# A four-layer graph network on one core: small products of TensorE cut into 64x64 blocks, one batch to a row half

## The chip, the cores and the metric

The kernel runs on one core of a Trainium2 chip. TensorE multiplies matrices into PSUM, VectorE and ScalarE work element by element, GpSimd and the sync engine (SP) issue most of the DMAs. The metric is the device time of the whole kernel in microseconds (us). Everything is fp32, except for masks in bf16.

## The reference

The input x has 8 batches of 2048 nodes with 64 features, and adj is one 2048x2048 matrix that all layers share. Each layer adds its result to its input and normalizes over the 64 features:

```python
x = _layernorm(x + _L0_gnn_ref(x, adj, embedding, weight, bias))   # x, A x, 2 A A x - x; weights per node
x = _layernorm(x + _L1_gnn_ref(x, adj, a))                         # attention, masked by adj, then elu
x = _layernorm(x + _L2_gnn_ref(x, adj, W, b))                      # (A + I)(x W^T + b) / row sum
x = _layernorm(x + _L3_gnn_ref(x, adj, iv, W1, b1, W2, b2, 0))     # three steps, below
```

A step of layer 3 forms `effects = adj @ v`, then `h = relu(concat(v, effects) @ W1.T + b1)` and `v = h @ W2.T + b2`. Four products by 64x64 matrices, or by a matrix of that size, matter here: layer 1's turn-back from features-by-nodes to nodes-by-features with its sum of weights, layer 2's W, the part of layer 3's step that prepares the input of the product with adj, and layer 3's last product with W2.

## The kernel before

Two batches lie side by side in the 128 columns or partitions: a *pair* p has 2 x 64 features, and there are four pairs (NPAIR). Nodes are cut into 16 tiles of 128 (NT) and into four *chunks* of 512 nodes (NCH, four tiles each, TPC). A sweep over adj is a product of a pair with the whole matrix: for each chunk, 16 products of 128x128 with 512 columns, summed in one PSUM tile `acc`.

Since a pair holds two batches, a product of 64x64 weights over its 128 partitions is written with a block-diagonal matrix of 128x128: the weights twice on the diagonal, zeros elsewhere. Such matrices are `w2bd` (layer 2), `w31e` and `ge` (layer 3's input), `w32c` (layer 3's last), and `back` (layer 1's turn-back: the identity, with two more columns that pick each batch's sum). The data are the stationary operand and the small matrix is the moving one. Each is used a chunk at a time:

- `finish` turns layer 1's result back, from `po`, which L889 fills: PSUM tile `pf`, 130 moving columns, two chunks per half of a pair
- `layer2_tail`: PSUM tile `ps_emb`, then VectorE scales, adds and normalizes
- `u_chunk`: PSUM tile `ps_u`, copied or added to a bias into the next sweep's source
- `last_chunk`, and `last_half` at the very end: PSUM tile `ps_v`, added to layer 3's result, normalized, stored

All of them go through `multiply` (L408 in the profile), which writes either one product with 128 output partitions (`PE`, the full form) or two with 64 each that run in two column tiles of the array (`PE columns`), by the form that the array is in. Layer 1's attention (`weights`, L889, `po`) always uses the column form. Layer 0's products (`second_pass`, L660, `yp`) use the row form (`PE rows`): 64 partitions of contraction, one batch to a row half, into the two halves of their PSUM tile.

The order of all instructions is fixed when the program is built. Each task is a Python generator that yields the engine that it needs next and the events that it waits for. `Plan` holds a clock for each engine, costs each piece by formulas (`mm`, `dve`, `act`), and always takes the task that could begin first, with an offset from the table `BACK` that is looked up by the task's name and pair. `Plan.run` adds `SWITCH` when TensorE's form changes. So costs and offsets shape the order on all engines, and the chip then runs that order, each engine waiting on semaphores. PSUM holds rings of tiles: `acc` (2), `pp` (2, all small products), `po` (1).

The main order on TensorE: two sweeps of layer 0 with `second_pass` between their products, then layer 2 and layer 3 of pairs 0 to 3 in turn, while layer 1 of the later pairs runs beneath them. The products of joined pairs use sums of quarters of adj (`joint_step`). SP fetches the tiles of adj into six buffers ahead of TensorE (`fetch`, L277).

Of the kernel before, what the change touches and what calls it, by code (L numbers as in the profile page):

```python
# [9 lines left out]
F32 = mybir.dt.float32  # L10
# [27 lines left out]
class Plan:  # L38
# [11 lines left out]
    FORMS = ("PE", "PE rows", "PE columns", "PE any")  # L50
    SWITCH = 0.2
# [4 lines left out]
        ("add_terms", 0): -3.73,  # L56
        ("h_evict", None): 0.94,
        ("keep", None): -0.94,
        ("last_chunk", None): -8.34,
        ("layer1", None): -0.21,  # L60
        ("mask_of_tile", None): -0.03,
        ("scores", 0): -0.81,
        ("scores", 2): 0.25,
        ("stacks", None): -0.5,
        ("start_chunk", None): -0.38,
        ("sweeps", None): 0.12,
# [29 lines left out]
    def either(self):  # L96
        return "PE" if self.form == "PE rows" else self.form
# [62 lines left out]
def mm(cols, n=1):  # L160

    return n * max(4 * cols / 2390, 0.224)
# [15 lines left out]
def resnorm_d4_kernel(  # L178
# [124 lines left out]
    blocks = ("w2bd", "w31v", "w31e", "w32c")  # L303
    w2bd, w31v, w31e, w32c = (const.tile([P, P], F32, name=n) for n in blocks)
    w32bd_t, w32bd_k = st_ring.take([P, 8, P], "w32bd")
    w32bd = w32bd_t[:, 0, :]
    for t in (a4, w2bd, w31v, w31e, w32bd, w32c):
        nc.vector.memset(t, 0.0)
# [6 lines left out]
    def constants():  # L315

        yield "PE", [40.0]
        nc.sync.dma_start(emb_sb, emb.rearrange("(t p) d -> p t d", p=P))
        nc.sync.dma_start(bias_sb, bias0)
        nc.sync.dma_start(embT, emb_t)  # L320
        halves = [slice(0, C), slice(C, P)]
        for k, w in enumerate((wk0, wk1, wk2)):
            for h in halves:
                nc.sync.dma_start(w[h, :], w0[k * C : (k + 1) * C, :])
        for k in range(2):
            for e in range(2):
                nc.sync.dma_start(a4[halves[e], 2 * k + e : 2 * k + e + 1], a1[halves[k], :])
        yield "PE", [70.0]
        nc.vector.tensor_tensor(wk0, wk0, wk2, ALU.subtract)
        nc.vector.tensor_scalar_mul(wk2, wk2, 2.0)  # L330
        plan.run("DVE", 2.0)
        plan.start(0, embedding_bias())
        yield "PE", [180.0]
        for t, src in (
            (w2bd, w2t),
            (w31v, w31t[0:C, :]),
            (w31e, w31t[C:P, :]),
            (w32bd, w32t),
            (w32c, w32t),
        ):  # L340
            for h in halves:
                nc.sync.dma_start(t[h, h], src)
        nc.sync.dma_start(b2b, b2.to_broadcast([P, C]))
        nc.sync.dma_start(b32b, b32.to_broadcast([P, C]))
        for h in halves:
            nc.sync.dma_start(b31b[h, :], b31)
            nc.sync.dma_start(b32c[h, :], b32.rearrange("o c -> c o"))
        nc.sync.dma_start(ivc, iv)
        yield "PE", [260.0]
        plan.start(0, weights_of_l23())  # L350
        for p in range(2, NPAIR):
            yield "SP", [(270.0, 430.0)[p - 2]]
            for c in range(NCH):
                load_x(p, c, nc.sync)
                at["x", p] = plan.dma("SP", 256)
# [4 lines left out]
    back = const.tile([P, P + 2], F32, name="back")  # L360
    nc.vector.tensor_copy(back[:, 0:P], ident)
    nc.vector.tensor_copy(back[:, P : P + 2], ident[:, C - 1 :: C])
    for e in range(2):
        rows = slice(e * C, (e + 1) * C)
        last = slice(e * C + C - 1, e * C + C)
        nc.vector.tensor_scalar_add(back[rows, last], ident[rows, last], -1.0)
# [4 lines left out]
    ge = const.tile([P, P], F32, name="ge")  # L371
# [38 lines left out]

    def embedding_bias():
        yield "PE", [pp_ring]
        pe, k = pp_ring.take([P, NT, C], "ps_eb")
        for t in range(NT):
            nc.tensor.matmul(
                pe[:, t, :], lhsT=embT[:, t * P : (t + 1) * P], rhs=bias_sb, start=True, stop=True
            )
        done = plan.run("PE", mm(C, NT))
        eng = yield EITHER, [done, e_ring]
        sb, ke = e_ring.take([P, NT, C], "eb_sb")  # L420
        copy(eng, sb, pe)
        done = plan.run(eng, cost(eng, 1024), done)
        pp_ring.give(k, done)
        e_ring.give(embT_k, plan.free["PE"])
        for e in range(2):
            nc.gpsimd.dma_start(eb[:, :, e, :], sb)
            done = plan.dma("DMA", 512, done)
        e_ring.give(ke, done)
        at["eb"] = done

    def weights_of_l23():
# [3 lines left out]
        for w, blocks in ((w2bd, 2), (w32c, 2), (b2b, 1), (b32b, 1)):  # L435
            mean = tiny([P, 1], "w_mean", 2)
            nc.vector.tensor_reduce(mean, w, AX.X, ALU.add)
            nc.vector.tensor_scalar_mul(mean, mean, 1.0 / C)
            for e in range(blocks):
                rows = slice(e * C, (e + 1) * C) if blocks == 2 else slice(0, P)  # L440
                block = w[rows, e * C : (e + 1) * C]
                nc.vector.tensor_scalar(block, block, mean[rows], None, ALU.subtract)
# [26 lines left out]
        for i, dst in enumerate((gv, ge, ceb)):  # L469
            nc.scalar.copy(dst, pw[:, i * P : (i + 1) * P])  # L470
        nc.scalar.activation(b31n, pw[:, 3 * P : 3 * P + 1], AF.Identity, bias=b31b)
# [54 lines left out]
    def layer_norm(v, n, after, centered=False):  # L526
# [4 lines left out]
        if not centered:  # L531
            yield "DVE", [after]
            s = tiny([P, nb], "ln_s", 4)
# [12 lines left out]
        vs = tiny([P, nb], "ln_v", 4)  # L546
# [5 lines left out]
        r = tiny([P, nb], "ln_r", 4)  # L552
        nc.scalar.activation(r, vs, AF.Ln)
        nc.scalar.activation(r, r, AF.Exp, scale=-0.5)
        rr = tiny([P, nb], "ln_rr", 2)
# [350 lines left out]
    def finish(p, h, po, kpo, xc):  # L906
# [11 lines left out]
        for f in range(2):  # L918
            yield "PE", [got, pp_ring]
            pp, k = pp_ring.take([P, 2, CW], "pf")  # L920
            pp = pp.rearrange("p b n -> p (b n)").rearrange("p (t n) -> p t n", n=256)
            for j in range(TPC):
                multiply(
                    pp[:, j, 0 : P + 2],
                    lhsT=poT[:, f, j * P : (j + 1) * P],
                    rhs=back,
                    start=True,
                    stop=True,
                )
            t_pe = plan.run("PE any", mm(P + 2, TPC), got)  # L930
            if f == 1:
                pt_ring.give(kt, t_pe)
            yield "DVE", [t_pe, hp_ring]
            rd = tiny([P, TPC, 2], "rd", 3)
            nc.vector.reciprocal(rd, pp[:, :, P : P + 2])
            hp, kh = hp_ring.take([P, CW], "hp")
            nc.vector.tensor_tensor(
                hp.rearrange("p (t e c) -> p t e c", e=2, c=C),
                pp[:, :, 0:P].rearrange("p t (e c) -> p t e c", c=C),
                rd.unsqueeze(3).to_broadcast([P, TPC, 2, C]),  # L940
# [65 lines left out]
    def h_evict(p, s, c, pa, ka, done):  # L1006
# [11 lines left out]
        if s < 2:  # L1018
            queue2.append(lambda: u_chunk(p, c, ge, u_of(p, s + 1), ceb, s + 1, done))
        else:  # L1020
            queue2.append(lambda: last_chunk(p, c, done))
# [9 lines left out]
    def layer2_tail(p, c, z, kz, done, ring=yt_ring):  # L1031
        yield "PE", [done, pp_ring]
        pe, k = pp_ring.take([P, TPC, P], "ps_emb")
        for j in range(TPC):
            multiply(
                pe[:, j, :], lhsT=z[:, j * P : (j + 1) * P], rhs=w2bd, start=True, stop=True
            )
        done = plan.run("PE any", mm(P, TPC), done)
# [4 lines left out]
        for j in range(TPC):  # L1043
            t = c * TPC + j
            nc.vector.scalar_tensor_tensor(
                v[:, j, :], pe[:, j, :], rdeg[:, t : t + 1], SX[p][:, t, :], ALU.mult, ALU.add
            )
# [8 lines left out]
    def start_chunk(p, c, v, done):  # L1056
# [21 lines left out]
        yield from u_chunk(p, c, w31e, u_of(p, 0), None, 0, done)  # L1078

    def u_chunk(p, c, w, dst, bias, s, done):  # L1080
# [4 lines left out]
        yield "PE", [done, pp_ring, *room]  # L1085
        pu, k = pp_ring.take([P, TPC, P], "ps_u")
        for j in range(TPC):
            multiply(
                pu[:, j, :], lhsT=SH_of[p][:, c * TPC + j, :], rhs=w, start=True, stop=True
            )  # L1090
        done = plan.run("PE any", mm(P, TPC), done)
        if bias is None:
            eng = yield EITHER, [done]
            copy(eng, dst[:, tiles(c), :], pu)
        else:
            eng = yield "DVE", [done]
            nc.vector.tensor_tensor(
                dst[:, tiles(c), :], pu, bias.unsqueeze(1).to_broadcast([P, TPC, P]), ALU.add
# [5 lines left out]
    def last_chunk(p, c, done):  # L1104
        yield "PE", [done, pp_ring]
        pv, k = pp_ring.take([P, TPC, P], "ps_v")
        for j in range(TPC):
            multiply(
                pv[:, j, :], lhsT=SH_of[p][:, c * TPC + j, :], rhs=w32c, start=True, stop=True
            )  # L1110
        done = plan.run("PE any", mm(P, TPC), done)
# [7 lines left out]
        nc.vector.tensor_tensor(v, v, pv, ALU.add)  # L1119
# [4 lines left out]
    def last_half(p, c, f, a, pa, done, token):  # L1124
# [13 lines left out]
        yield "PE", [done, pp_ring]  # L1138
        pv, k = pp_ring.take([P, 2, P], "ps_v")
        for j in range(2):  # L1140
            multiply(pv[:, j, :], lhsT=h[:, j, :], rhs=w32c, start=True, stop=True)
        done = plan.run("PE any", mm(P, 2), done)
# [4 lines left out]
        nc.vector.tensor_tensor(v, v, pv, ALU.add)  # L1147
# [469 lines left out]
```

## Time and profile before

| | |
|---|---|
| runs, us | 2055.12, 2055.51, 2056.45; median 2055.51 |
| profiled execution: span, us | 2054.9 (0.6 under the median; the page gives no other time for it) |
| TensorE busy | 2013.2 us, 98% of the span |
| VectorE busy | 1472.5 us, 72% |
| ScalarE busy | 975.7 us, 47% |
| GpSimd busy | 310.1 us, 15% |
| DMA | 522.81 MB moved, mean 254 GB/s |
| granted TensorE clock | 0.996 on average |

A line of the profile names the line of the kernel, the engine, the operation, the tile written and the tiles read, the shapes and the count. L408 is the helper `multiply`, so products are told apart by the PSUM tile. An fp32 product of the program appears as two MATMUL records, each with a weight load (LDWEIGHTS). `128*128` before the shapes are the active rows and columns of the array: `64*128` is the row form, `128*64` the column form. A record's length includes the time until its result is through, so records overlap; the distance between starts is the rate. A group's idle time is put down to what ended it.

### The profile page before, as it was taken

Reading aid. Unit: us, or ns where it says so; the run is one execution under the profiler, and the core shown is the slowest. Engines: PE = TensorE matmul, PEld = TensorE weight load, DVE = VectorE, ACT = ScalarE, POOL = GpSimd, SP = SyncE. Lnnn points to the kernel's source line nnn. Section 1 sums busy time; section 2 is a strip of 40 time slices with the busy share of each in tenths; the row PEclk is TensorE's granted clock in tenths of the full one; section 3 lists DMA queues with packets and bytes.
Section 4 is the critical chain, followed back from the end, with each engine's and each line's share of the span. In section 5 each row is a group of like instructions: output and inputs, shape, how many; then the busy total and the mean of one; then the engine's idle time right before and its main releaser. Section 6 shows DMA issues by size and latency. Waiting matters only on the chain. (4 is left out here: it accounts for less than half of the span.)

```text
span 2054.9 us, 22213 instructions
## 1 busy us (share of the span) xinstructions
PE 2013.2 (98%) x7835; PEld 889.4 (43%) x7835; DVE 1472.5 (72%) x1906; ACT 975.7 (47%) x1786; POOL 310.1 (15%) x491
## 2 busy tenths in 40 slices
PE   8999999999999999999998999999999999999998
PEld 3444444443343443444333343453344554444444
DVE  2215666999899999979999989999989832121214
ACT  0014444288778546767773846623767521000002
POOL 3220111122222331222211101001101000000000
PEclk9999999999999999999999999999999999999999
DMA  9897776676657789967778779779777677888886
GB/s 297 285 306 257 285 274 231 214 225 174 166 156 234 185 282 324 282 224 272 206 219 318 246 244 347 247 257 359 245 273 259 224 249 262 267 270 267 265 283 197
DMA packets 205714, 522.81 MB, mean 254 GB/s; under 512 B 22290, under 2 KB 29074, under 8 KB 201490
## 3 DMA queue, kind: packets, MB, share of 16 engines
q1 hardware_dynamic: 151570, 352.60, 50.5%
q0 software_dynamic: 51920, 167.74, 27.5%
q8 instruction: 62, 1.02, 0.2%
q10 hardware_dynamic: 2112, 1.05, 0.2%
q14 instruction: 50, 0.41, 0.1%
HBM read 488.61 MB, written 64.16 MB: 269 GB/s over the span
## 5 line engine op out<-in xcount | busy, mean ns | idle before, releaser
L408 PE MATMUL acc<-a,SX 128*128 128x512 f32 (+1 forms) x1372 | 493.6, 597 | 11.4 <-DMA SX<-in_x 6.9
L408 PE MATMUL acc<-a,SB 128*128 128x512 f32 (+2 forms) x1120 | 375.9, 588 | 3.3 <-DMA a<-a_plus_i 2.7
L870 ACT ACTIVATE e<-e,sv 128x1024 f32<-128x1024 f32 x256 | 280.7, 1153 | 70.6 <-DVE e L862 67.8
L408 PEld LDWEIGHTS acc<-a,SX 128*128 128x128 f32 (+1 forms) x1372 | 192.5, 170 | 269.5 <-issue 255.0
L684 ACT ACTIVATE terms<-yp,emb_sb 128x128 f32<-128x128 f32 x896 | 243.0, 396 | 133.8 <-PE yp L660 128.3
L862 DVE TENSOR_TENSOR e<-s1b,mk 128x2048 f32<-128x2048 f32 x128 | 290.1, 2283 | 7.6 <-PE po L889 4.2
L784 DVE CUSTOM_DVE_ANT_0 junk<-s2b,mr 128x2048 bf16<-128x2048 f32 x128 | 292.6, 2286 | 2.3 <-DMA mr<-by_row 0.5
L875 DVE TENSOR_TENSOR e<-e,mb 128x2048 f32<-128x2048 f32 x128 | 290.6, 2284 | 4.1 <-ACT e L870 3.9
L878 ACT ACTIVATE e<-e 128x2048 f32<-128x2048 f32 x128 | 245.7, 1926 | 90.6 <-DVE e L875 89.8
L889 PE MATMUL po<-e,SX 128*64 128x512 f32 x1024 | 232.5, 595 | 3.0 <-ACT e L878 3.0
L408 PEld LDWEIGHTS acc<-a,SB 128*128 128x128 f32 (+1 forms) x1120 | 147.3, 164 | 194.9 <-issue 186.8
L408 PE MATMUL acc<-a,SA 128*128 128x512 f32 (+1 forms) x416 | 176.4, 598 | 4.5 <-DMA a<-in_adj_t 4.5
L857 POOL DMA_DIRECT2D mk<-by_col x128 | 70.8, 560 | 497.9 <-DVE e L862 446.8
L660 PE MATMUL yp<-SH,xgT 64*128 64x512 f32 x512 | 137.2, 613 | 3.4 <-ACT terms L684 3.3
L696 DVE TENSOR_TENSOR terms<-terms 128x512 f32<-128x512 f32 (+1 forms) x176 | 130.0, 739 | 12.0 <-ACT terms L684 7.6
L889 PEld LDWEIGHTS po<-e,SX 128*64 128x64 f32 x1024 | 72.7, 137 | 150.4 <-issue 139.8
L660 PE MATMUL yp<-wk,xgT 64*128 64x512 f32 x512 | 131.8, 592 | 0.0
L660 PE MATMUL yp<-SH,y2T 64*128 64x512 f32 x512 | 131.2, 589 | 0.0
L408 PEld LDWEIGHTS acc<-a,SA 128*128 128x128 f32 (+1 forms) x416 | 70.0, 183 | 90.4 <-issue 87.5
L408 PE MATMUL acc<-a,ut 128*64 128x512 f32 (+1 forms) x272 | 86.4, 593 | 1.4 <-DVE wk L1356 1.4
L408 PE MATMUL acc<-a,t 128*128 128x512 f32 x192 | 85.3, 592 | 0.0
L771 POOL DMA_DIRECT2D mr<-by_row x64 | 34.6, 542 | 294.3 <-DVE mx L784 253.7
(255 smaller groups left out, 1716.0 us busy)
## 6 DMA issues: line engine op xcount, KB each, us to landing
a<-in_adj_t SPq DMA_DIRECT2D x384, 512.0 KB, 5.9
a<-a_plus_i SPq DMA_DIRECT2D x88, 512.0 KB, 5.2
mr<-by_row POOLq DMA_DIRECT2D x64, 512.0 KB, 5.8
mk<-by_col POOLq DMA_DIRECT2D x128, 256.0 KB, 5.8
a<-sb SPq DMA_DIRECT2D x40, 512.0 KB, 4.4
a<-sc SPq DMA_DIRECT2D x40, 512.0 KB, 4.5
a<-sd SPq DMA_DIRECT2D x40, 512.0 KB, 5.1
a<-sa SPq DMA_DIRECT2D x40, 512.0 KB, 4.3
```

The costliest lines, as they stand in the source:

```text
L408: nc.tensor.matmul(out[h], lhsT=lhsT[:, h], rhs=rhs, skip_group_check=True, **kw)
L660: nc.tensor.matmul(yp[:, e, :], lhsT=v[rows, cs], rhs=w[rows, hs], start=(k3 == 0), stop=(k3 == 2),)
L684: nc.scalar.activation(batches(terms[0][:, dd, :]), term, AF.Copy, scale=weight)
L696: nc.vector.tensor_tensor(a, a, b, ALU.add)
L771: nc.gpsimd.dma_start(mk, by_row[t])
L784: nc.vector.tensor_tensor_reduce(out=junk, in0=s2b[e][0], in1=masks[t][0], scale=1.0, scalar=LOWEST, op0=ALU.add, op1=ALU.max, accum_out=m ...
L857: nc.gpsimd.dma_start(mk, by_col[jt // 2][:, jt % 2, h * HALF : (h + 1) * HALF])
L862: nc.vector.tensor_tensor(e, s1b[0], mk.unsqueeze(1).to_broadcast([P, 2, HALF]), ALU.add)
L870: nc.scalar.activation(e[:, i, :], e[:, i, :], AF.Prelu, bias=sv[:, 2 + i, jt : jt + 1], alpha=ALPHA)
L875: nc.vector.tensor_tensor(e, e, mb[0], ALU.add)
L878: nc.scalar.activation(e, e, AF.Exp)
L889: nc.tensor.matmul(po[i * C : (i + 1) * C, f, :], lhsT=SX[p][:, t, i * C : (i + 1) * C], rhs=e[:, i, f * CW : (f + 1) * CW], start=(t == 0 ...
```

## The change

The four kinds of small product no longer use block-diagonal matrices. The matrix is kept twice, one below the other, as [128, 64] (`w2q`, `w31q`, `w32q`, `geq`, and `back` with 65 columns), one copy for each batch's 64 partitions. The new helper `quarters` multiplies in blocks of 64x64: for each tile of 128 nodes, four products, with e the batch (the row half of the array) and f the half of the nodes (the column half). Each batch writes its own half of the PSUM tile, so the evictions read views split by batch. The plan has a new form, `PE quarters`, at 0.112 us for each tile of nodes, the cost of a change of form is set to 0.1 instead of 0.2, the table `BACK` has new offsets, most of them by pair, and some small rings of the norm are deeper.

```diff
-    FORMS = ("PE", "PE rows", "PE columns", "PE any")
-    SWITCH = 0.2
+    FORMS = ("PE", "PE rows", "PE columns", "PE quarters", "PE any")
+    SWITCH = 0.1
...
     BACK = {
-        ("add_terms", 0): -3.73,
-        ("h_evict", None): 0.94,
...
-        ("last_chunk", None): -8.34,
...
+        ('add_eb', 2): 7.7,
+        ('add_terms', 0): -34.15,
...
+        ('mask_of_tile', 2): 24.71,
...
+        ('z_and_v', 3): -21.09,
     }
...
     def either(self):
-        return "PE" if self.form == "PE rows" else self.form
+        return self.form if self.form == "PE columns" else "PE"
...
-    blocks = ("w2bd", "w31v", "w31e", "w32c")
-    w2bd, w31v, w31e, w32c = (const.tile([P, P], F32, name=n) for n in blocks)
+    w31v, w31e = (const.tile([P, P], F32, name=n) for n in ("w31v", "w31e"))
+    w2q, w31q, w32q, geq = (const.tile([P, C], F32, name=n) for n in ("w2q", "w31q", "w32q", "geq"))
...
-            (w2bd, w2t),
             (w31v, w31t[0:C, :]),
             (w31e, w31t[C:P, :]),
             (w32bd, w32t),
-            (w32c, w32t),
         ):
             for h in halves:
                 nc.sync.dma_start(t[h, h], src)
+        for t, src in ((w2q, w2t), (w31q, w31t[C:P, :]), (w32q, w32t)):
+            for h in halves:
+                nc.sync.dma_start(t[h, :], src)
...
+    def quarters(out, source, w, width=C):
+
+        n = source.shape[1] // P
+        for j in range(n):
+            for e, f in ((0, 0), (1, 1), (0, 1), (1, 0)):
+                rows = slice(e * C, (e + 1) * C)
+                nc.tensor.matmul(
+                    out[f * C : (f + 1) * C, e, j * width : (j + 1) * width],
+                    lhsT=source[rows, j * P + f * C : j * P + (f + 1) * C],
+                    rhs=w[rows],
+                    start=True,
+                    stop=True,
+                    skip_group_check=True,
+                )
+
+    def quartered(n):
+
+        return 0.112 * n
...
-        for w, blocks in ((w2bd, 2), (w32c, 2), (b2b, 1), (b32b, 1)):
+        for w in (w2q, w32q, b2b, b32b):
...
-        for i, dst in enumerate((gv, ge, ceb)):
+        for i, dst in ((0, gv), (2, ceb)):
             nc.scalar.copy(dst, pw[:, i * P : (i + 1) * P])
+        for e in range(2):
+            block = slice(e * C, (e + 1) * C)
+            nc.scalar.copy(geq[block, :], pw[block, P + e * C : P + (e + 1) * C])
...
-            s = tiny([P, nb], "ln_s", 4)
+            s = tiny([P, nb], "ln_s", 6)
...
-            yield "PE", [got, pp_ring]
+            yield "PE quarters", [got, pp_ring]
             pp, k = pp_ring.take([P, 2, CW], "pf")
-            for j in range(TPC):
-                multiply(
-                    pp[:, j, 0 : P + 2],
-                    lhsT=poT[:, f, j * P : (j + 1) * P],
-                    rhs=back,
...
+            quarters(pp, poT[:, f, :], back, C + 1)
...
-        yield "PE", [done, pp_ring]
-        pe, k = pp_ring.take([P, TPC, P], "ps_emb")
-        for j in range(TPC):
-            multiply(
-                pe[:, j, :], lhsT=z[:, j * P : (j + 1) * P], rhs=w2bd, start=True, stop=True
-            )
-        done = plan.run("PE any", mm(P, TPC), done)
+        yield "PE quarters", [done, pp_ring]
+        pe, k = pp_ring.take([P, 2, CW], "ps_emb")
+        quarters(pe, z, w2q)
+        done = plan.run("PE quarters", quartered(TPC), done)
...
-        pu, k = pp_ring.take([P, TPC, P], "ps_u")
-        for j in range(TPC):
-            multiply(
-                pu[:, j, :], lhsT=SH_of[p][:, c * TPC + j, :], rhs=w, start=True, stop=True
-            )
-        done = plan.run("PE any", mm(P, TPC), done)
+        pu, k = pp_ring.take([P, 2, CW], "ps_u")
+        quarters(pu, SH_of[p][:, tiles(c), :].rearrange("p t n -> p (t n)"), w)
+        pu = pu[:, :, 0 : TPC * C].rearrange("p e (t c) -> p e t c", c=C)
+        to = by_batch(dst[:, tiles(c), :])
+        done = plan.run("PE quarters", quartered(TPC), done)
...
-        nc.vector.tensor_tensor(v, v, pv, ALU.add)
+        nc.vector.tensor_tensor(by_batch(v), by_batch(v), pv, ALU.add)
```

The products of `last_chunk` and `last_half` change in the same way as `u_chunk`'s.

## The prediction

> **What bounds the kernel now.** I read first the page's busy times and slices, then the busy time of each 100 us, then TensorE's own waits, and last the order of time at a few small products and at changes of form.
>
> ```profile
> PE 2013.2 (98%) x7835; PEld 889.4 (43%) x7835; DVE 1472.5 (72%) x1906; ACT 975.7 (47%) x1786; POOL 310.1 (15%) x491
> ...
> DVE  2215666999899999979999989999989832121214
> ```
>
> TensorE works 98% of the span, so it sets the end. VectorE is nearly as full from slice 8 to 31 (about 400 to 1640 us), and idle after that. So an edit to VectorE's work counts only in the middle, and an edit to TensorE's counts everywhere, as long as VectorE keeps up there. Per 100 us:
>
> ```profile
> 1400.00:1500.00 100.00, 95.53 (x413) 34.46 (x413) 96.37 (x60) 64.71 (x52) 12.97 (x24) 1.00 0.86 306
> ...
> 1700.00:1800.00 100.00, 100.00 (x282) 48.18 (x281) 21.80 (x42) 9.43 (x19) 0.00 (x0) 1.00 0.81 267
> ```
>
> The columns are busy us of TensorE, its weight loads, VectorE, ScalarE, GpSimd, then TensorE's clock and the DMA share. From 1000 to 1500 TensorE loses 14.5 us, the most of any such stretch; from 1700 to 2000 it loses none. Its own waits from 1000 to 1500 are split between adjacency tiles (7.2 us) and results of ScalarE and VectorE (7.2 us in six rows), of which the largest are:
>
> ```profile
> PE acc L408 <- DMA a<-in_adj_t: 4.1, 3, 1.8
> PE acc L408 <- DMA a<-a_plus_i: 3.1, 3, 1.5
> PE po L889 <- ACT e L878: 3.0, 2, 1.8
> ```
>
> Now the price of a small product and of a change of form. In the timeline of TensorE the columns are start, length, what it is, and the count; each fp32 product of the program is two MATMUL records per tile of the array.
>
> ```profile
> 1366.56 1.05 PE L408 MATMUL ps_u<-ge,SH 128*128 128x128 f32 x8
> 1367.45 2.31 PE L408 MATMUL acc<-a,SB 128*128 128x512 f32 x5
> ...
> 795.75 1.04 PE L408 MATMUL ps_emb<-w2bd,z 128*64 128x128 f32 x16
> 796.63 1.89 PE L408 MATMUL acc<-a,SX 128*64 128x512 f32 x8
> ...
> 502.68 0.58 PE L408 MATMUL ps_sv<-a,xT 128*64 128x4 f32 x16
> ...
> 435.51 1.45 PE L408 MATMUL acc<-a,SB 128*128 128x512 f32 x3
> 436.90 0.70 PE L660 MATMUL yp<-SH,xgT 64*128 64x512 f32 x2
> ...
> 438.72 1.02 PE L660 MATMUL yp<-SH,y2T 64*128 64x512 f32 x4
> 439.67 1.55 PE L408 MATMUL acc<-a,SX 128*128 128x512 f32 x3
> ...
> 515.94 1.45 PE L408 MATMUL acc<-a,SA 128*128 128x512 f32 x3
> 517.32 1.94 PE L889 MATMUL po<-e,SX 128*64 128x512 f32 x8
> ```
>
> A chunk of four tiles takes 0.89 us in the full form (1366.56 to 1367.45) and 0.88 in the column form (795.75 to 796.63). The last three pairs are changes of form. Three records of acc are 0.429 us apart (1.45 less one record's 0.592, halved), so the rows' first record was due at 436.80 and came at 436.90, and its pair lasts 0.70 where later pairs last 0.59: entering rows costs 0.10 + 0.10 = 0.20 us. Back into full: due at 439.58, came at 439.67, and three records take 1.55 where they took 1.45: again 0.20. Into columns: due 517.23, came 517.32, and eight records take 1.94 where they take 1.89 without a change: 0.145. So each form has to let the last one end and then shows its first weight load, 0.10 for 128 columns and 0.05 for 64.
>
> **The chunks.** By the groups of TensorE kept apart by shape, ps_u has 288 full and 192 column records, ps_emb 80 and 96, ps_v 72 and 112, pf 88 and 80; at 8 and 16 records that is 66 full and 30 column chunks, 96 in all (two of layer 3's last come as halves, so 97 visits). They cost 66 x 0.89 + 30 x 0.88 = 85.1 us. The new chunk has 16 products of 64x64x64, 32 records. No row shows four tiles at once. The nearest is ps_sv above: 64-column weights, two tiles at once, almost no moving columns; its fifteen starts take 0.58 - 0.195 (one record) = 0.385, and a steady round of two takes 0.0585 by their start times, so one load of 64 columns takes a round. The moving side, half of a 128-column record's 0.111, is 0.055 and hides beneath it. Bounds: four tiles a round give 8 rounds, 0.468 us; two a round, as in every row here, give 16 rounds, 0.936. I take the first: rows (yp) and columns (po) each run their two tiles with starts 0.007 apart (the pair of yp at 436.90 lasts 0.70, one record 0.693), the new blocks combine the two, and the two row halves write different halves of the PSUM tile, as yp's do. 96 x 0.468 = 44.9, a gain of 40.2 us.
>
> The Trainium skill (TensorEngine Tiling, Instruction Overhead) speaks against it: a matmul has about 60 cycles of overhead, so a moving side of 64 should not be tiled further. Its page TensorE: Matmul & The Clock Gate (Wait — 56ns, not 53.3ns?) gives a floor of about 25 ns from start to start; by that a chunk is an estimated 0.80 us, 96 of them cost 32 us more than I count, and the change would lose about 15. The ps_sv row, 0.385 over fifteen starts, cannot tell this floor from its two-tile rounds; starts 0.007 apart in yp say that it isn't one for neighbouring tiles.
>
> **The changes of form.** Before, a chunk takes the form that stands (only rows are left for full), so most change nothing. After, every visit enters and leaves. Keeping the order of before, the 97 visits are 85 runs of neighbouring chunks: 85 entries x 0.145 = 12.3; 61 exits to full or rows x 0.20 = 12.2; 23 to columns x 0.145 = 3.3; less 8 changes that stood there already (1.6). That costs 26.2 us. The rest is 40.2 - 26.2 = 14.0 us gained: some 3 before 1000 us, 7.5 to 1640, 3.5 after. An isolated chunk between full products gains only 0.89 - 0.468 - 0.345 = 0.08.
>
> **The rest of the edits.** The evictions keep their 512 elements a partition. Their views are split by batch; the row of hp<-pf,rd, already split four ways, has 691 ns against 687 of the contiguous sum with ps_v, so nothing, covered by VectorE's 74 us idle from 400 to 1600 us; without that cover 64 times 4 ns is 0.3 us. Set-up: two block loads more on SP (0.48 to 0.59 us each at 183.7), ahead of the next adjacency tiles; at most 1.2 us if TensorE waited for exactly these, and I take none, since SP stood idle for 22 us before them. ScalarE gets one small copy more at about 262 us, VectorE two subtractions of 0.25 and two memsets fewer. Deeper rings of the norm's small tiles let more norms be open and cost no instruction.
>
> **The order.** The new table of offsets rewrites the order on every engine, and the trace can't show it. Best: the 7.2 us of waits for ScalarE and VectorE go, and some twenty visits stand next to another (0.345 each), together -14. Worst: TensorE loses in each 100 us from 1000 to 1600 what it lost in 1400 to 1500 (4.5), 27 where it lost 14.5: +12.5. I take -3: the plan now counts a change of form as 0.1, the rows say 0.145 to 0.20, so TensorE runs behind its plan by some 20 us in all and finds results ready more often. For tiles from HBM nothing changes.
>
> **Sum.** 2054.9 is the span of the profiled execution, 0.6 under the median of the runs, and I count against the median: 2055.5 - 14.0 - 3 = 2038.5.
>
> **Rivals.** (1) Fewer than four tiles at once, or a floor for each matmul. A chunk loses from 0.89 - 26.2/96 = 0.61 us up, that is below three tiles a round; at two, 96 x 0.468 = 44.9 more: 2083. For it: no row with more than two; against: the starts 0.007 apart. (2) VectorE becomes the bound up to 1640 us: what is gained there is given back, only 3.5 us remain, 2052, no change that can be told (within 0.2%, 4 us, is about that). For: 96% busy in the window of 1400 us; against: its 74 us idle. (3) Four at once, but the new order makes TensorE wait, +12.5 instead of -3, and as many more form changes as it gained in clustering is lost on row products: about 2060. For: 0.1 in the plan is too low; against: it makes TensorE late, not early. (4) The order brings all of its 14: 2027, or still more visits side by side, down to 2015.
>
> **How the numbers follow.** The forecast with its own range 2026 to 2049 has 0.54; more than that by the order (4) 0.13; no change (2) 0.08; slower by the order (3) 0.08; tiles not at once (1) 0.17. Faster 0.67, same 0.08, slower 0.25. Four cases in five lie between 2016 and 2076, short of the worst of (1).
>
> **What would show it.** Right: a chunk in 64*64 records, 32 of them, within about 0.5 us of its first start, four starts within 0.03; about 0.145 lost before it and 0.2 after it; VectorE's evictions at their old 687 to 691 ns; TensorE's busy time about 14 us down, its idle not up. Wrong: 0.8 us or more from the first 64*64 start to the last; TensorE's idle over 55 us; VectorE without idle from 1000 to 1640. The forecast falls with the first of these.

## The result and the profile after

The changed kernel takes 2072.04 us (median, 2069.01 to 2073.29) where the kernel before takes 2055.32 beside it: a ratio of 1.0084, 95% interval 1.0062 to 1.0107. It is slower by about 17 us; the forecast was 17 us faster. The profiled execution took 2073.19 us, with a span of 2071.4. From the page:

```profile
span 2071.4 us, 25804 instructions
...
PE 2008.1 (97%) x9623; PEld 855.2 (41%) x9623; DVE 1471.7 (71%) x1903; ACT 976.9 (47%) x1788; POOL 309.5 (15%) x491
...
DVE  2215756998799999989999989999989721111124
```

TensorE is busy 5.1 us less than before (2013.2). But the span less the busy time is now 63.3 us, where it was 2054.9 - 2013.2 = 41.7: 21.6 more, and 21.6 - 5.1 = 16.5 is the whole loss. VectorE's row of slices and its busy time are nearly those of before, so VectorE was not made slower. The busy time per stretch (columns as in the prediction) says where the idle time lies:

```profile
1400.00:1500.00 100.00, 92.96 (x439) 35.30 (x441) 98.09 (x63) 64.99 (x54) 14.59 (x27) 1.00 0.82 290
1700.00:1800.00 100.00, 96.80 (x441) 43.25 (x440) 19.89 (x37) 8.88 (x19) 0.00 (x0) 1.00 0.79 257
1800.00:1900.00 100.00, 96.73 (x405) 42.65 (x404) 16.54 (x25) 5.63 (x9) 0.00 (x0) 1.00 0.79 257
```

In 1400 to 1500 TensorE loses 2.6 us more than before. From 1700 to 2000, where it had lost nothing, it now loses 3.2 in each 100 us, while VectorE is busy 20%: it waits for an engine that has little to do. TensorE's own waits from 1640 us to the end name what it waits for (total, times, longest):

```profile
PE acc L452 <- DVE u L1419: 4.9, 6, 0.9
PE acc L452 <- DVE u L1425: 4.7, 6, 0.8
PE ps_v L469 <- ACT h_o L1198: 1.1, 1, 1.1
PE acc L452 <- DVE u3t L1432: 0.8, 1, 0.8
PE acc L452 <- DVE c L1194: 0.5, 1, 0.5
```

Before, the same stretch has two waits, 2.0 us in all:

```profile
PE ps_v L408 <- ACT h_o L1135: 1.4, 1, 1.4
PE acc L408 <- DVE c L1131: 0.6, 1, 0.6
```

L1419 is `x_of` and L1425 is `z_and_v`, the subtractions on VectorE in layer 3's joint steps of pairs 2 and 3. One such place in the timeline, with a chunk of `ps_u` ahead of it:

```profile
1741.65 0.59 PE L452 MATMUL acc<-a,t 128*128 128x512 f32 x1
...
1742.17 0.69 PE L469 MATMUL ps_u<-geq,SH 64*64 64x64 f32 x32
...
1742.80 7.13 PE L452 MATMUL acc<-a,u3t 128*128 128x512 f32 x16
...
1749.97 0.69 DVE L1419 TENSOR_TENSOR u<-acc,u 128x512 f32<-128x512 f32 x1 [6.34 <-PE acc L452]
...
1750.71 7.13 PE L452 MATMUL acc<-a,u3t 128*128 128x512 f32 x16 [0.78 <-DVE u L1419]
...
1757.96 0.69 DVE L1419 TENSOR_TENSOR u<-acc,u 128x512 f32<-128x512 f32 x1 [7.29 <-PE acc L452]
...
1758.70 5.42 PE L452 MATMUL acc<-a,SB 128*128 128x512 f32 x12 [0.85 <-DVE u L1419]
```

Two things are to be read here. First the chunk: its 32 records of 64*64 take 0.52 us from the start of the last full record to their first start (0.429 was due, so 0.09 goes to letting the array empty), and the next full record starts 0.63 later. By the start times of the records the 32 lie within 0.477 us; three of every four gaps between neighbours are 7 ns or less, and the mean is 15.4 ns. So four blocks do run at once. The second full record of acc comes 0.105 us late (0.534 after the first instead of 0.429), its weight load exposed. A visit that stands alone costs 0.823 against 0.89 before.

Second, the wait. `acc` has two tiles. At 1742.80 a product of 16 records fills one; it is read by VectorE at 1749.97 for 0.69 us; only then does the next product start, at 1750.71, and the next one waits for `x_of` in the same way. Three products in a row use one and the same tile, while the other one is not used. The waits for `z_and_v` are alike: there TensorE adds a product to the tile that VectorE has only just read. The twelve make 9.6 us.

The end has changed, too. The last product of TensorE and what follows:

```profile
2057.36 0.46 PE L469 MATMUL ps_v<-w32q,h_o 64*64 64x64 f32 x16 [1.12 <-ACT h_o L1198]
...
2060.18 1.13 ACT L614 ACTIVATE ln_sq<-SX 128x512 f32<-128x512 f32 x2
...
2064.30 0.69 DVE L633 TENSOR_TENSOR SX<-SX,ln_r 128x512 f32<-128x512 f32 x1
...
2066.29 0.75 POOL L1225 DMA_DIRECT2D out<-SX  x1 [0.25 <-DVE SX L633]
```

After the last small half (128x256) the norms of whole chunks of 512 columns, whose products ran from 2033.4 to 2049.5 us, still come one after another on ScalarE and VectorE, and the last store is issued 8.5 us after TensorE's last product ended. From there to the end of the span it is 13.6 us in all; before it was 6.3.

### The profile page after: what moved, and what is told of

It is laid out like the page before. It is cut to its first block, busy times and chain, and to the rows that moved or that the text cites. A ratio compares the mean times of both kernels' runs of the same rounds, so it can differ in the third digit from the quotient of the medians.

```text
span 2071.4 us, 25804 instructions
## 1 busy us (share of the span) xinstructions
PE 2008.1 (97%) x9623; PEld 855.2 (41%) x9623; DVE 1471.7 (71%) x1903; ACT 976.9 (47%) x1788; POOL 309.5 (15%) x491
## 4 chain that ended last, share of the span: by engine, by line
PE 67%; issue 22%; DVE 6%; DMA 2%; ACT 2%; POOL 0%; POOLq 0%; DVEq 0%; ACTq 0%; SPq 0%
PE acc L452 39%; PE yp L731 16%; PE po L960 9%; DVE e L933 2%; DVE e L946 1%; DVE junk L855 1%; DMA a<-in_adj_t 1%; ACT terms L755 1%; PE ps_sv L452 1%; ACT e L941 1%; PE ps_u L469 0%; DMA a<-a_plus_i 0%; PE pf L469 0%; PE ps_xg L685 0%; PE ps_xT L795 0%
## 5 line engine op out<-in xcount | busy, mean ns | idle before, releaser
L452 PE MATMUL acc<-a,SX 128*128 128x512 f32 (+1 forms) x1300 | 494.9, 598 | 14.5 <-DMA a<-in_adj_t 6.9
L452 PE MATMUL acc<-a,SB 128*128 128x512 f32 (+2 forms) x1004 | 381.4, 594 | 3.9 <-DVE u L1419 1.6
L452 PE MATMUL acc<-a,ut 128*128 128x512 f32 (+1 forms) x212 | 87.0, 597 | 0.0
```

What stands on the lines that cost most here:

```text
L452: nc.tensor.matmul(out[h], lhsT=lhsT[:, h], rhs=rhs, skip_group_check=True, **kw)
```

## The experiments

One table for all, in us. Ratio: to the kernel before, with its 95% interval. The other columns are from each kernel's profiled execution: the joint stage is from the end of the last `ps_emb` product to TensorE's last record (layer 3 of pairs 2 and 3 together), the step is one of its three; the tail is from that record to the end of the span; idle is TensorE's between its first and last record; changes are changes of form in TensorE's order, leaving out a few small set-up products (how these are classed moves a count by a few), with an estimate of their cost at 0.145 us into columns and blocks and 0.20 into full and rows.

| kernel | median | ratio | span | joint stage | step | tail | idle | changes (us) |
|---|---|---|---|---|---|---|---|---|
| before | 2055.5 | 1 | 2054.9 | 332.6 | 110.1 | 6.3 | 28.5 | 132 (24.8) |
| after | 2072.0 | 1.0084 [1.0062, 1.0107] | 2071.4 | 344.5 | 113.9 | 13.6 | 43.1 | 314 (55.4) |
| same order | 2039.4 | 0.9924 [0.9906, 0.9941] | 2042.2 | 330.9 | 109.6 | 6.6 | 27.9 | 293 (51.1) |
| order only | 2085.2 | 1.0142 [1.0121, 1.0164] | 2083.2 | 346.1 | 114.5 | 13.5 | 42.9 | 160 (29.7) |
| one offset less | 2063.6 | 1.0037 [1.0023, 1.0050] | 2061.1 | 336.9 | 111.7 | 13.6 | 36.2 | 314 (55.4) |
| three offsets less | 2049.6 | 0.9985 [0.9975, 0.9996] | 2043.5 | 330.9 | 109.6 | 6.4 | 31.3 | 315 (55.4) |
| plan with true prices | 2056.4 | 1.0010 [0.9998, 1.0023] | 2057.0 | 334.9 | 109.6 | 6.4 | 31.4 | 332 (58.9) |
| before + three offsets | 2073.3 | 1.0089 [1.0074, 1.0104] | 2071.9 | 346.1 | 114.5 | 14.5 | 37.0 | 132 (24.8) |
| old table | 2078.2 | 1.0114 [1.0095, 1.0133] | 2075.5 | 330.9 | 109.6 | 6.4 | 49.5 | 329 (58.1) |

**The blocks in the order of before.** The changed kernel's products, with the plan, the prices, the table and the rings of before. The plan is told that nothing has changed, so the products keep their places: in the traces the order of TensorE's products is that of before from the first to the last.

```diff
-    FORMS = ("PE", "PE rows", "PE columns", "PE quarters", "PE any")
-    SWITCH = 0.1
+    FORMS = ("PE", "PE rows", "PE columns", "PE any")
+    SWITCH = 0.2
...
-        ('add_eb', 2): 7.7,
...
+        ("add_terms", 0): -3.73,
...
-        yield "PE quarters", [done, pp_ring]
+        yield "PE", [done, pp_ring]
...
-        done = plan.run("PE quarters", quartered(TPC), done)
+        done = plan.run("PE any", mm(P, TPC), done)
```

> The 64x64 blocks of the changed kernel, issued in the order of the kernel before: the plan's costs, forms, offsets and ring depths of before, so that only the products, their weights and the views of the evictions are new. Theory A (the blocks gain what the rows say, and the new order loses it): a visit between full products costs 0.093 + 0.477 + 0.148 + 0.105 = 0.82 us in the changed kernel's trace where it was 0.89, one between column products about 0.75 where it was 0.88; over the 85 runs of chunks of the old order some 12 us, so 2043 us, between 2038 and 2048. Theory B (the blocks themselves cost it: TensorE's changes of form delay what other engines wait for): 2060 us or more, slower than before.

Measured: 0.9924, some 16 us faster than before. The page, and TensorE's waits from 1620 us to the end:

```profile
PE 2001.0 (98%) x9899; PEld 844.2 (41%) x9899; DVE 1471.1 (72%) x1904; ACT 974.9 (48%) x1787; POOL 310.0 (15%) x491
```

```profile
PE ps_v L425 <- ACT h_o L1154: 1.3, 1, 1.3
PE acc L408 <- DVE c L1150: 0.6, 1, 0.6
PE ps_vT L1093 <- DVE ln_v L587: 0.3, 1, 0.3
```

TensorE's busy time is 12.2 us under that of before, its idle time the same, and no wait for `x_of` or `z_and_v` is left. So the products are worth about what they were forecast to be, and the loss lies in the order. This kernel beats both.

**The order alone.** The products of before, with the plan, prices, table and rings of the changed kernel. In the traces TensorE's order is that of the changed kernel from the first product to the last.

```diff
-    SWITCH = 0.2
+    SWITCH = 0.1
...
-        ("add_terms", 0): -3.73,
...
+        ('add_eb', 2): 7.7,
...
-        done = plan.run("PE any", mm(P, TPC), done)
+        done = plan.run("PE quarters", quartered(TPC), done)
```

> The order of the changed kernel (its forms, costs, offsets and ring depths in the plan), with the old block-diagonal products of 128x128. Theory A: the new order alone loses about 27 us, and the blocks take some 12 to 14 of them back, so without them it is slower than the changed kernel: 2072 + 13 = 2085 us, between 2078 and 2092. Theory B: the order is as good as the old one, and without the blocks the time falls back to 2055 to 2062.

Measured: 1.0142, 29 us slower. With 128x128 products the same waits stand in the joint stage, to the tenth:

```profile
PE acc L452 <- DVE u L1404: 4.9, 6, 0.9
PE acc L452 <- DVE u L1410: 4.7, 6, 0.8
```

(L1404 and L1410 are `x_of` and `z_and_v` here.) From this kernel to the changed one it is 1.0084 / 1.0142, about 12 us gained by the blocks; from the blocks in the old order to the changed kernel it is 1.0084 / 0.9924, 33 us lost by the order. Both ways, the order costs about 30.

**One offset less.** The entry that puts layer 3's `h_evict` of pair 2 back by 18.55 us is the nearest suspect for the `acc` tile, since `h_evict` gives its tile back at its end, and `Ring.take` hands out the tile that the plan has as free first.

```diff
-        ('h_evict', 2): 18.55,
```

> The changed kernel without one entry of its table of offsets, that of h_evict for pair 2 (18.55). Theory A: with the entry, the plan gives the second acc tile back 18.55 us late in its order of decisions, so three steps of layer 3 use one acc tile where they have two, and TensorE waits 0.8 us for VectorE at each of 12 products (9.6 us in its waits on u). Without it these waits go: 2062 us, between 2058 and 2066. Rival: these waits only stand in the place of others behind them (results of VectorE in the same step), and the time stays within 3 us of 2072.

Measured: 1.0037, 2063.6 us, in the range of theory A, though only half of what it named went. The six waits for `x_of` are gone, those for `z_and_v` are left:

```profile
PE acc L451 <- DVE u L1424: 4.7, 6, 0.8
PE ps_v L468 <- ACT h_o L1197: 1.1, 1, 1.1
PE acc L451 <- DVE c L1193: 0.5, 1, 0.5
```

A step falls from 113.9 to 111.7 us. By the ratios this entry, one number, costs 1.0084 - 1.0037, about 10 us. The spans of the two profiled executions are 10.3 apart, and the joint stage has 7.6 of that. The rest lies ahead of it, where TensorE, VectorE and ScalarE run the same order in both kernels, so it is a difference of executions: the last `ps_emb` ends at 1713.3 us in one and at 1710.6 in the other. In the changed kernel's timeline ScalarE reads the other tile for `h_evict` until 1742.97, long before 1750.71:

```profile
1742.28 0.69 ACT L1072 ACTIVATE SH<-acc,b31b 128x512 f32<-128x512 f32 x1 [7.04 <-PE acc L452]
```

So on the chip that tile is free. It is the order of the program that does not use it.

**Three offsets less.** The two other entries that name what is late: `z_and_v` of pair 3, put forward by 21.09, so that TensorE takes the product that adds to z's tile as soon as it is asked for, and stands until VectorE has read that tile; and `store` of pair 3, put back by 3.79, so that the norms of whole chunks come after the last half chunk.

```diff
-        ('h_evict', 2): 18.55,
...
-        ('store', 3): 3.79,
...
-        ('z_and_v', 3): -21.09,
```

> The changed kernel without three entries of its table: h_evict for pair 2 (as in the run before), z_and_v for pair 3 (-21.09) and store for pair 3 (3.79). Theory: beside the acc tile, z_and_v's offset lets TensorE take the seeded product of layer 3 before VectorE has written z (4.7 us of waits on u left in the run without h_evict's entry, 0.8 at each of six products), and store's offset puts three norms of pair 3 behind the very last half chunk, so that 13.6 us pass from TensorE's last product to the end, where the old order has 6.7. Without all three: 2063.6 - 4.7 - 6.9 = 2052 us, between 2048 and 2056, which leaves some 12 us to the blocks in the old order (2039.4) for the time before layer 3's joint steps and the changes of form. Rival: the end and the seeds are not on the path, and the time stays above 2060.

Measured: 2049.55, 0.9985. The waits after 1640 us are those of before, the step is 109.6, the tail 6.4:

```profile
PE ps_v L466 <- ACT h_o L1195: 1.3, 1, 1.3
PE acc L449 <- DVE c L1191: 0.6, 1, 0.6
```

The three entries cost 1.0084 - 0.9985, 20 us, more than the whole loss. `z_and_v` and `store` were taken out together; what each does is told apart by place, the joint stage (336.9 to 330.9) and the tail (13.6 to 6.4).

**The three offsets in the kernel before.** Are they bad in themselves, or only beside blocks that end earlier?

```diff
         ("h_evict", None): 0.94,
+        ("h_evict", 2): 18.55,
+        ("z_and_v", 3): -21.09,
+        ("store", 3): 3.79,
```

> The kernel before, with its block-diagonal products, and with the three entries of the new table added (h_evict for pair 2, z_and_v and store for pair 3). If these three cost what they cost by their place in layer 3 and at the end, whatever the products are: 9 us from the acc tile, 5 from the seeds, 7 from the end, so some 20 us more than before, 2075 us (2068 to 2080). If they hurt only together with the blocks (because these are shorter or change the form), less than 8 us more, below 2064.

Measured: 1.0089, 18 us slower, with no 64x64 product in the kernel and the prices of before. The waits from 1640 us on:

```profile
PE acc L411 <- DVE u L1359: 4.9, 6, 0.9
PE acc L411 <- DVE u L1365: 4.7, 6, 0.8
PE ps_v L411 <- ACT h_o L1138: 1.1, 1, 1.1
```

They are bad by their place, whatever the products are.

**The old table under the new prices.** The changed kernel with its own prices (0.112 for a tile, 0.1 for a change of form) and the table of before.

```diff
-        ('add_eb', 2): 7.7,
-        ('add_terms', 0): -34.15,
...
-        ('z_and_v', 3): -21.09,
+        ("add_terms", 0): -3.73,
+        ("h_evict", None): 0.94,
...
+        ("sweeps", None): 0.12,
```

> The changed kernel with the table of offsets of before, and with the new plan's prices (0.112 for a tile in blocks, 0.1 for a change of form). If the new table was the only fault, this keeps the blocks' gain: 2045 or less. If any order that the plan makes under its new prices differs enough from the old one to lose it (the plan's own end is 2065 here, with some 290 changes of form priced 0.045 to 0.1 too low): 2070 to 2090.

Measured: 1.0114. The joint stage and the tail are as good as in the best kernel (330.9 and 6.4), but the last `ps_emb` comes at 1738.3 us instead of 1713.3, and TensorE idles 49.5 us:

```profile
PE acc L408 <- DMA a<-in_adj_t: 14.1, 10, 2.6
PE ps_vT L1093 <- DVE SX L589: 8.9, 2, 4.6
...
PE po L916 <- ACT e L905: 4.9, 1, 4.9
```

So it is not the table alone. A table fits one set of prices; with other prices the same offsets give another order, here a worse one in the first 1700 us.

**A plan with true prices.** The plan was given what the traces show: 0.2 for a change into full or rows, 0.145 into columns and blocks, 0.1175 a tile, and the waits that it did not charge, for a free PSUM tile and for the product that `z_and_v` adds. The table was then fitted anew to the plan's own end.

```diff
-    SWITCH = 0.1
+    SWITCH = {"PE": 0.2, "PE rows": 0.2, "PE columns": 0.145, "PE quarters": 0.145}
...
         self.t = self.freed.pop(k)
+        if self.plan:
+            self.plan.free["PE"] = max(self.plan.free["PE"], self.t)
...
-        return 0.112 * n
+        return 0.1175 * n
...
                 seeded(p, 2 + k, pa, False)
                 done = plan.free["PE"] + plan.LAG
+                plan.free["PE"] = max(plan.free["PE"], done)
```

> The changed kernel with a plan that counts what the traces show: a change of form 0.2 into full and rows, 0.145 into columns and blocks, a chunk in blocks 0.47, and the waits for PSUM tiles and for the seeds. Its table of offsets is made anew, for the end of the plan. Theory: the plan was misled by its prices, and told the right ones it finds an order that keeps the blocks' gain; its own end is 2039.8, so between 2034 and 2050 us, below both kernels. Rival: the plan misses the chip by more than these prices (the changed kernel's plan ended at 2031 for 2072), and the new order falls back above 2055.

Measured: 2056.42, 1.0010: not the 2034 to 2050 of the first theory, but above 2055 as the rival said. The joint steps and the tail are those of the best kernel, but there are long waits elsewhere:

```profile
PE acc L495 <- DMA a<-in_adj_t: 11.2, 4, 4.1
...
PE ps_vT L1180 <- DVE v L1171: 3.5, 2, 3.0
...
PE ps_vT L1180 <- DVE SX L676: 3.2, 1, 3.2
```

They cost more than they last. In the lines around the wait of 4.1 us, TensorE's busy time is the first number after the comma, and its granted clock is the third from the end:

```profile
1406.00:1408.00 2.00, 1.69 (x4) 0.38 (x2) 0.70 (x3) 0.00 (x0) 0.53 (x1) 1.00 0.97 359
1408.00:1410.00 2.00, 0.00 (x0) 0.00 (x0) 0.09 (x1) 0.00 (x0) 0.00 (x0) 1.00 1.03 402
1410.00:1412.00 2.00, 0.20 (x1) 0.20 (x2) 2.00 (x1) 0.00 (x0) 0.00 (x0) 0.66 1.04 414
1412.00:1414.00 2.00, 2.00 (x3) 0.96 (x4) 2.00 (x2) 1.76 (x2) 0.54 (x1) 0.50 1.03 395
1414.00:1416.00 2.00, 2.00 (x3) 0.50 (x3) 2.00 (x2) 1.99 (x3) 0.54 (x1) 0.50 1.02 388
1416.00:1418.00 2.00, 2.00 (x4) 0.63 (x2) 2.00 (x3) 0.62 (x1) 0.00 (x0) 0.63 1.04 389
1418.00:1420.00 2.00, 1.74 (x4) 0.68 (x4) 2.00 (x2) 1.15 (x1) 0.00 (x0) 1.00 1.04 386
```

For 7 us after the wait TensorE works at half clock, which makes 3.4 us more, counted as busy. Adding up one minus the clock over slices of 1 us up to TensorE's last work, this execution loses 17.1 us in seven such spells, against 3.4 in two with the three offsets less. That difference, 13.7, is as large as the difference of their spans, 2057.0 - 2043.5 = 13.5. But these are one of the longer executions of the one and the shortest of the other: the medians are only 6.9 apart. The granted clock averages 0.9925 over eleven timed executions of this kernel and 0.9953 over twelve of the other, which makes an estimated 5.5 us of about 2050, so the clock is most of that difference too. The plan knows nothing of the clock.

## Why the prediction was wrong

**What bounds the kernel**: right. TensorE is busy 97 to 98% of the span in all kernels here. One reading in this step is not so: 1000 to 1500 us, with 14.5 us lost, is not the worst such stretch, since 0 to 500 loses 17.6.

**The chunks** (0.468 us, 40.2 us gained): right. A chunk takes 0.477 from the first start to the last, so four tiles a round, and 96 of them 45.8 us instead of 44.9. The floor of 25 ns from start to start, which the Trainium skill gives (TensorE: Matmul & The Clock Gate, Wait — 56ns, not 53.3ns?), does not hold between blocks in different tiles of the array: 15.4 ns is the mean over 32 starts. Nor does its advice to take no tiling factor from a dimension that is already small (TensorEngine Tiling, Instruction Overhead), which I held against a moving side of 64, decide here: a chunk fell from 0.89 to 0.477.

**The changes of form** (0.145 in, 0.20 out; 26.2 us more): right in the order that the step spoke of. The same-order kernel has 293 changes where before has 132, 161 more as forecast (85 + 61 + 23 - 8), at those prices 51.1 - 24.8 = 26.3. An isolated visit gains 0.067 (0.89 - 0.823), forecast 0.08.

**Their sum** (-14.0): the same-order kernel gained 15.6 by its ratio (0.0076 x 2055.5; 12 to 19 by the interval). The granted clock averages 0.9964 in its five executions and 0.9955 in the fourteen of the kernel before, so an estimated 2 of the 15.6 are the clock, which no step counted.

**The other edits** (nothing): in the changed kernel VectorE's evictions of `ps_u` and `ps_v` take 684 to 689 ns (before 685 to 691), those of `ps_emb`, a quarter as long, 337 to 340 (before 338 to 343), and its busy time is 0.8 us less than before. Right.

**The order** (-3, bounds -14 and +12.5): wrong, and this is the step that failed. It is worth about +29 with the products of before and about +33 with the blocks. Two things in it were wrong. The worse bound was taken from 1000 to 1600 us alone, because there the trace showed waits. From 1700 to 2000 TensorE lost nothing before, so I priced nothing there, though an order that is rewritten can put a wait anywhere: it put 9.6 us there, and 7.3 us more into the tail, which no step spoke of. And the reason for -3, that TensorE behind its plan finds results ready more often, speaks of engines that run ahead freely. It does not hold where the order binds TensorE to what VectorE does with the tile that TensorE has just written: twelve products of the joint stage then wait 0.8 us each, however late TensorE is.

Rival (3) had the right mechanism, a new order that makes TensorE wait, but with 0.08 and at 2060 it was held for too rare and too cheap. The argument against it, that too low a price for a change of form makes TensorE late and not early, was the same error. What was to show it wrong, idle of over 55 us (63.3 by the span, where before has 41.7), did show. Rival (1), tiles not at once, and rival (2), VectorE as the bound, fell with the records and with the same-order kernel.

Where the 29.2 us lie between the spans of the same-order kernel and the changed one: the last `ps_emb` comes 8.6 us later, the joint stage is 13.6 longer, the tail 6.9. For the second and third the cause is shown, by taking the three offsets out (back to 330.9 and 6.4) and by putting them into the kernel before (to 346.1 and 14.5). For the first it is in part: 21 changes of form more (4.3 us), and the wait for `ut`, 3.0 us at 1595, which stands in all four kernels with this order up to there (the changed one, the order alone, one and three offsets less), each time with a spell of half clock after it (1.7 us), and in none of the others. But single executions differ as much: with the same order up to there, the last `ps_emb` ends at 1713.3, 1710.6 and 1706.1 us in the changed kernel and with one and three offsets less. Between the kernel with three offsets less and the same-order kernel there remain 0.9985 - 0.9924, 12 us by the timed runs. In their profiled executions, without the half-clock spells (3.4 and 10.2), it is 2040.1 - 2032.0 = 8.1; 4.3 of changes of form and 3.4 of idle time make 7.7 of that. By the mean granted clock of the timed executions (0.9953 and 0.9964) an estimated 2 us more are the clock. What is left of the 12 stays open.

## What to carry to other kernels

When an edit changes both the instructions and the order in which a planner puts them, run the two apart: here the products gained 16 us and the order lost some 30, and neither shows in the sum. A rewritten order is a risk in the stages where the trace is clean, because a single offset can bind a full engine to one PSUM tile; price it by going through each ring of few tiles and asking which task gives a tile back late. And do not carry offsets fitted to one set of prices over to another: the old table under the new prices (1.0114) and three offsets of the new table under the old prices (1.0089) both made a slower kernel.

## What the runs showed of the hardware that I had not expected

**A wait of TensorE can cost nearly twice its length.** In the nine profiled executions, from 100 us on, I added up TensorE's idle time over neighbouring slices of 1 us that are idle for more than 0.3 us. All 12 such gaps of 3.7 us and more were followed by TensorE at half clock within 8 us, of 10 gaps from 2.8 to 3.3 us 6 were, and of 47 from 1.5 to 2.7 us 10. A spell lasts about 3.4 or 6.8 us and takes 1.7 or 3.4 us. In the changed kernel after the wait of 3.0 us for `ut`:

```profile
1594.00:1596.00 2.00, 1.35 (x8) 0.21 (x4) 2.00 (x2) 1.39 (x2) 0.00 (x0) 1.00 0.01 4
1596.00:1598.00 2.00, 0.00 (x0) 0.00 (x0) 2.00 (x2) 1.71 (x2) 0.00 (x0) 1.00 0.80 246
1598.00:1600.00 2.00, 1.62 (x6) 0.78 (x8) 1.93 (x6) 2.00 (x2) 0.00 (x0) 0.69 0.04 16
1600.00:1602.00 2.00, 2.00 (x7) 0.65 (x5) 1.97 (x4) 1.76 (x8) 0.00 (x0) 0.50 0.00 0
1602.00:1604.00 2.00, 2.00 (x12) 0.73 (x10) 1.86 (x6) 0.09 (x1) 0.00 (x0) 0.96 0.04 5
```

The Trainium skill describes a gate that halves TensorE's clock after an idle window of about 3.4 us, with windows that run freely (TensorE: Matmul & The Clock Gate, Part 1: The HAM clock gate (the "warmup" mystery)); the traces agree on the halving, on the length (spells of 3.41 and 6.83 us), and in that gaps near 3 us halve it in one place and not in another. They do not agree that it takes a whole idle window: gaps of about 2 us were followed by half clock too. So twelve waits of 0.8 us cost 9.6, with no such spell after them in the changed kernel, and a single one of 4 us costs an estimated 5.7 to 7.4. The spells lose 6.8 us in the kernel before, 8.5 in the changed one, and 17.1 each with the old table and with the true prices; these two have single waits of 4.9 and 4.1 us after 1100 us, where the kernel before has none over 1.8.

**Four 64x64 blocks of fp32 run at once**, with starts 7 ns apart, and what they cost beside is the change of form: 0.346 us in and out together (0.823 - 0.477), of the 0.413 (0.89 - 0.477) that a lone chunk saves.
